# A sixteen-head, six-layer local-attention kernel: all scores of a half step in one run, the values of both heads in one run at its end, v's pieces together, k's norms of the second half in mid-step

## The chip, the cores and the metric

The kernel runs on one core of a Trainium2 chip. The time is device microseconds of that core for one execution of the whole program. The core has five engines with a queue each: PE (matrix products), DVE (vector work), ACT (activations and copies), POOL (more vector work) and SP, which here does nothing but issue DMAs. An engine takes its queue in order: an instruction that waits holds up all those behind it.

## The reference, cut to what matters

Sixteen sequences of 256 tokens with 128 features go through one causal attention layer (stage one of the kernel, which the change does not touch) and then through six layers of local attention and a gated feed-forward block (stage two):

```python
for i in range(DEPTH):                       # 6 layers
    x = attn_layer(shift_tokens(x), Wqkv[i], q_scale[i], k_scale[i], Wo[i]) + x
    x = ffn_layer(shift_tokens(x), ln_g[i], ln_b[i], W1[i], b1[i], W2[i], b2[i]) + x

# attn_layer: 16 heads of 64 features, windows of 32 tokens
q = l2norm(q) * qs;  k = l2norm(k) * ksc
q = q * cos * scale + rotate_half(q) * sin * scale
k = k * cos / scale + rotate_half(k) * sin / scale
sim = einsum('bhwie,bhwje->bhwij', bq, look(bk)) * 8   # own window and the one before
attn = softmax(where(mask, -max, sim), -1)
out = einsum('bhwij,bhwje->bhwie', attn, look(bv))
```

`look` joins each window with the window before it. All of it is in 32-bit floats.

## The kernel before, in words

Stage two handles 96 items n (six layers times sixteen sequences), one step each. A step has two halves, u = 0 and u = 1. Around item n the steps are a software pipeline: in step n the kernel projects q and k of item n + 2 (`proj_qk`, L463 to L477), finishes the norms of item n + 1 (`sums`, `roots`, `spread_k`, `norm_k`), computes the scores of item n (`sim`, L583), and projects the attention's result of item n - 1 (`project_out`, L666, which the profile calls wo). The heads are taken in four groups g of four (NG = 4); in every half, two of the four score tiles of an item, i = 2u and j = 2u + 1, are handled. The feed-forward block takes two sequences at a time (512 columns), spread over two steps: `glu_shift`, `glu_center` (cen), `glu_var` (pv), `glu_norm` (rs), `glu_part` (hg, ha) and `glu_out` (w). Which of them stands in a half depends on whether n is even, so the pattern repeats every pair of steps, that is every four halves.

The parts that the change and the prediction touch:

- `proj_qk` makes a PSUM tile `qk`; ACT squares it (L464), DVE multiplies it by the rotary tables into `t` (L465), POOL adds squares and turned parts (L474, L477) into `sq` and `tq`.
- `sums` (called n in the profile) adds the squares on PE (L484) and ACT copies the sums out. `roots` transposes them (nT, L495); DVE takes the inverse root in eleven small operations (nx, then rn and nz, L499 to L508); POOL spreads the result (kb, L511).
- `spread_k` transposes kb to a PSUM tile bc (L522), two groups at a time. `norm_k` multiplies the two k tiles by it on DVE (L536) and issues four DMAs on SP (L538) from `tq` to `us`, the layout that the scores read. `us` has three buffers.
- `masks` writes the mask into the PSUM tile of the scores (L563), `sim` adds the products of one group (64 small matmuls of two groups come to about 0.8 us). `soften` scales by q's and k's roots and subtracts the maximum (DVE L595, L603, POOL L604), `power` is the exponential (ACT, L610), `share` divides by the sum (DVE L617, L618; L620 on POOL or DVE).
- `attn_T` transposes the weights (aT, L626, copied by ACT at L628), `attn_v` multiplies by the values (po, L646, copied by ACT at L655).
- `proj_v` makes one of two pieces c of v for half u (v, L546); ACT copies it to `vn`, and SP issues DMAs that move it by one window to `vs` (L553, and for c = 0 also L555). `attn_v` reads both.

The order of the work is written out by hand in `half`. `in_order` pins it on PE, DVE, ACT and POOL: each instruction there gets an order-only dependence on the one before it on its engine. SP is not pinned; the framework's planner places the DMAs, and weight loads come as early as their buffers allow. PSUM tiles come from two pools: four slots for everything that `psum1` makes, two wider ones for scores and values (`psum2`). A tile waits for the last reader of the tile that had its slot.

Of the kernel before, what the change touches and what calls it, by code (L numbers as in the profile page):

```python
# [21 lines left out]
NG = HEADS // 4  # L22
# [16 lines left out]
def tile_transformer(  # L39
# [316 lines left out]
    with ExitStack() as st:  # L356
# [18 lines left out]
        def psum1(name):  # L375
            return ps_o.tile([P, 512], F32, tag="o", name=name)
# [115 lines left out]
        def roots(n, n2):  # L492
            ps = psum1(f"nT_{n}").rearrange("p (h g m) -> p h g m", h=4, g=4)
            for h in range(2):
                nc.tensor.transpose(  # L495
                    ps[:, h].rearrange("p g m -> p (g m)"), n2[:, h].rearrange("p a m -> p (a m)"), ident
                )
            x = p2.tile([P, 2, NG, 8], F32, tag="nx", name=f"nx_{n}")
            nc.vector.tensor_scalar(x, ps[:, 0:2, :, 0:8], 1e-24, None, ALU.max)  # L499

            y = p3.tile([P, 2, NG, 8], F32, tag="rn", name=f"rn_{n}")
            x_, y_ = (v.rearrange("p h g m -> p (h g m)") for v in (x, y))
            nc.vector.tensor_scalar(y_.bitcast(I32), x_.bitcast(I32), -0.5, 1597463007.0, ALU.mult, ALU.add)
            for _ in range(3):
                z = p4.tile([P, 64], F32, tag="nz", name=f"nz_{n}")
                nc.vector.tensor_tensor(z, x_, y_, ALU.mult)
                nc.vector.scalar_tensor_tensor(z, z, -0.5, y_, ALU.mult, ALU.mult)
                nc.vector.scalar_tensor_tensor(y_, z, 1.5, y_, ALU.add, ALU.mult)  # L508
            rn[n] = y
            kb = p1.tile([P, 2, NG, P], F32, tag="kb", name=f"kb_{n}")  # L510
            nc.gpsimd.tensor_copy(  # L511
                kb.rearrange("p h g (i d) -> p (h g) i d", d=32),
                y.rearrange("p h g m -> p (h g) m")[:, :, 4:8].unsqueeze(3).to_broadcast([P, 8, 4, 32]),
            )
            kbs[n] = kb
# [160 lines left out]
        def glu_shift(m):  # L676
            b = m % 8
            x2 = x2s[m] = p1.tile([P, 2 * S], F32, tag="gl", name=f"x2_{m}")
            for i in range(2):
                shifted(x2[:, i * S : (i + 1) * S], 2 * b + i)  # L680

        def glu_center(m):
            x2 = x2s.pop(m)
            ps = psum1(f"cen_{m}")
            nc.tensor.matmul(ps, center, x2, start=True, stop=True)
            sq2 = p1.tile([P, 2 * S], F32, tag="h1", name=f"fsq_{m}")
            nc.scalar.activation(sq2, ps, AF.Square)
            xc = p1.tile([P, 2 * S], F32, tag="h2", name=f"xc_{m}")
            nc.scalar.copy(xc, ps)
            xns[m] = sq2, xc  # L690

        def glu_var(m):
            sq2, xc = xns[m]
            pv = psum1(f"pv_{m}")
            for t in range(4):
                nc.tensor.matmul(pv[:, t : t + 1], sq2[:, t * P : (t + 1) * P], mean1, start=True, stop=True)
            var = p4.tile([P, 4], F32, tag="var", name=f"var_{m}")
            nc.vector.tensor_scalar(var, pv[:, :4], 1e-5, None, ALU.add)
            rstd = p4.tile([P, 4], F32, tag="rstd", name=f"rstd_{m}")
            rsqrt(rstd, var)  # L700
            xns[m] = rstd, xc

        def glu_norm(m):
            l = m // 8
            rstd, xc = xns[m]
            ps = psum1(f"rs_{m}")
            for t in range(4):
                nc.tensor.matmul(
                    ps[:, t * P : (t + 1) * P],
                    rstd[:, t : t + 1].to_broadcast([P, P]),  # L710
                    ident,
                    start=True,
                    stop=True,
                    is_transpose=True,
                )
            xn = p1.tile([P, 2 * S], F32, tag="xn", name=f"xn_{m}")
            nc.vector.tensor_tensor(xn, ps, xc, ALU.mult)
            nc.gpsimd.tensor_scalar(xn, xn, vecs[:, l, V_G : V_G + 1], vecs[:, l, V_B : V_B + 1], ALU.mult, ALU.add)
            xns[m] = xn

        def glu_part(mm, i):
            l = mm // 8
            if mm % 8 == 0 and i == 0:
                load_glu(l)
            xn = xns[mm]
            a, m = DI_PARTS[i]
            pg, ph = psum1(f"hg_{mm}_{i}"), psum1(f"ha_{mm}_{i}")
            nc.tensor.matmul(pg[:m], W["1"][:, DI + a : DI + a + m], xn, start=True, stop=True)  # L728
            nc.tensor.matmul(ph[:m], W["1"][:, a : a + m], xn, start=True, stop=True)  # L729
            g = p1.tile([P, 2 * S], F32, tag="gl", name=f"g_{mm}_{i}")  # L730
            nc.scalar.activation(g[:m], pg[:m], AF.Gelu, bias=vecs[:m, l, V_B1 + 3 + i : V_B1 + 4 + i])
            h = p1.tile([P, 2 * S], F32, tag=f"h{i}", name=f"h_{mm}_{i}")
            nc.vector.scalar_tensor_tensor(
                h[:m], ph[:m], vecs[:m, l, V_B1 + i : V_B1 + i + 1], g[:m], ALU.add, ALU.mult
            )
            hs[mm, i] = h
# [8 lines left out]
        def leave(s):  # L745

            ps = psum1(f"fin_{s}")
            for t in range(2):
                c0 = (s % 2) * S + t * P
                nc.tensor.transpose(ps[:, t * P : (t + 1) * P], yT[s // 2][:, c0 : c0 + P], ident)  # L750
            res = p2.tile([P, 2, E], F32, tag="res", name=f"res_{s}")
            nc.sync.dma_start(res, out[s].rearrange("(t p) e -> p t e", p=P))
            nc.vector.tensor_tensor(res, ps[:, :S].rearrange("p (t e) -> p t e", t=2), res, ALU.add)
            nc.sync.dma_start(out[s].rearrange("(t p) e -> p t e", p=P), res)
# [6 lines left out]
        def has(n):  # L761
            return 0 <= n < N

        def do(n, f, *a):
            if has(n):
                f(n, *a)
# [6 lines left out]
        def half(n, u):  # L773
            even = n % 2 == 0
            m = n // 2 - 1 if even else (n - 3) // 2
            glu = lambda m: 0 <= m < N // 2
            i, j = 2 * u, 2 * u + 1
            b, bu = (n, 0) if u else (n - 1, 1)
            bi, bj = 2 * bu, 2 * bu + 1
            do(b, share, bi)  # L780
            do(b, share, bj)
            do(n, sim, u, 0)
            do(n, sim, u, 1)
            for k in range(2):
                do(n + 2, proj_qk, i, k)
            if u == 0:
                do(n + 1, sums)
            elif not even and glu(m):
                glu_norm(m)
            do(n, sim, u, 2)  # L790
            do(n, sim, u, 3)
            do(n, soften, i)
            do(n, soften, j)
            do(n - 1, project_out, u)
            if u:
                do(n + 3, shift)
                if even and glu(m):
                    glu_shift(m)
            elif has(n + 1):
                roots(n + 1, n2s.pop(n + 1))  # L800
            do(b, attn_T, bi)
            do(b, attn_T, bj)
            do(n, proj_v, u, 0)
            do(b, attn_v, bi)
            if not even and u == 0 and glu(m):
                glu_center(m)
            do(n + 2, proj_qk, j, 0)
            if even and u == 0 and glu(m - 1):
                glu_part(m - 1, 2)
            if not even and glu(m):  # L810
                if u == 0:
                    glu_var(m)
                else:
                    glu_part(m, 0)
                    glu_part(m, 1)
            do(n + 2, proj_qk, j, 1)
            do(n + 1, spread_k, u)
            do(n + 1, norm_k, u)
            do(n, power, i)
            do(n, power, j)  # L820
            do(b, attn_v, bj)
            do(*((n, masks, 1) if u == 0 else (n + 1, masks, 0)))
            if even and u and glu(m - 1):
                glu_out(m - 1)
                if m - 1 >= (DEPTH - 1) * 8:
                    leave(2 * ((m - 1) % 8))
                    leave(2 * ((m - 1) % 8) + 1)
            do(n, proj_v, u, 1)

        last = {}  # L830
# [17 lines left out]
        for n in range(-2, N + 3):  # L848
            for u in range(2):
                traced = len(nc.cur_bb.bb.instructions)  # L850
                half(n, u)
                in_order(traced, 0 <= n < N)
# [97 lines left out]
```

## Time and profile before

| | |
|---|---|
| Median of 3 runs | 3765.55 us (3759.4 to 3772.61) |
| Profiled execution | 3770.29 us, span 3768.5 us |
| Granted TensorE clock, mean | 0.981 |
| PE busy | 3540.0 us, 94% |
| DVE busy | 2782.3 us, 74% |
| POOL busy | 2537.4 us, 67% |
| ACT busy | 1889.9 us, 50% |
| DMA, mean rate | 88 GB/s |
| PE idle before sim, until `us` landed | 107.2 us in 62 waits |

Stage one and the change to stage two take about the first 450 us; from there on the pattern of four halves repeats. A busy time is the sum over an engine's instructions; waits are given with the instruction that waited, and the one whose end released it. A pair of steps can be read half by half from the first `sim` of one half to the first `sim` of the next.

### The profile page before, as it was taken

The page shows a single profiled execution, that of the slowest core. Times are in us where ns is not written, and L with a number is a line of the kernel's source. Part 1 is how long each engine was busy: PE and PEld are TensorE (multiplying, and loading weights), DVE is VectorE, ACT ScalarE, POOL GpSimd, SP SyncE. Part 2 cuts the span into 40 slices and gives each one's busy share as a digit, 9 for nine tenths or more (in the row PEclk, how much of TensorE's full clock was granted, in tenths as well). Part 3 has the DMA queues.
Part 4 walks back from the last instruction along what each step waited for, and adds up shares of the span by engine and source line. Part 5 has one row for each costly group of instructions (what it writes and reads, how often), then busy time and mean ns, then how long its engine had stood idle before and what let it go on. Part 6 is the DMA issues. An engine that isn't in the chain of part 4 may idle for free.

```text
span 3768.5 us, 153634 instructions
## 1 busy us (share of the span) xinstructions
PE 3540.0 (94%) x68032; PEld 2482.4 (66%) x68032; DVE 2782.3 (74%) x4882; ACT 1889.9 (50%) x3180; POOL 2537.4 (67%) x2667
## 2 busy tenths in 40 slices
PE   8888799999999999999999999999999999999998
PEld 6666566666666666666666666666666666666665
DVE  5455677887877887777877778887777787777773
ACT  4444345555555554555554555555555555555453
POOL 1000577777777777777777777777777777777772
PEclk9999899999999999999999999999999999999998
DMA  2000233334333334333334333334333343333332
GB/s 79 6 8 8 68 99 84 97 96 105 105 93 96 88 95 106 103 95 86 96 99 105 94 102 88 93 94 105 105 87 96 86 104 93 107 91 96 102 96 63
DMA packets 249445, 331.66 MB, mean 88 GB/s; under 512 B 74446, under 2 KB 105548, under 8 KB 247884
## 3 DMA queue, kind: packets, MB, share of 16 engines
q1 hardware_dynamic: 248060, 321.13, 31.9%
q8 instruction: 536, 8.78, 1.0%
q14 instruction: 129, 1.06, 0.1%
q10 hardware_dynamic: 720, 0.70, 0.1%
HBM read 28.12 MB, written 4.19 MB: 9 GB/s over the span
## 4 chain that ended last, share of the span: by engine, by line
PE 75%; DMA 10%; DVE 5%; ACT 4%; issue 2%; POOL 2%; SPq 1%; ACTq 0%; DVEq 0%; POOLq 0%
PE qk L463 16%; PE po L646 9%; PE wo L666 9%; PE v L546 8%; DMA us<-tq 7%; PE sim L583 6%; PE w L742 4%; DMA vs<-vn 3%; PE hg L728 3%; PE ha L729 3%; PE aT L626 3%; PE bc L522 2%; PE st L222 1%; SPq L538 1%; ACT ex L269 1%
## 5 line engine op out<-in xcount | busy, mean ns | idle before, releaser
L465 DVE TENSOR_TENSOR t<-qk,ab 128x1024 f32<-128x1024 f32 x768 | 916.1, 1218 | 411.3 <-ACT sq L464 364.9
L477 POOL TENSOR_TENSOR tq<-t 128x512 f32<-128x512 f32 x768 | 961.0, 1272 | 105.9 <-DVE t L465 66.0
L463 PE MATMUL qk<-xs,wqk 128*128 128x256 f32 x3072 | 789.3, 393 | 0.4 <-DVE yT L671 0.2
L474 POOL TENSOR_TENSOR sq<-sq 128x512 f32<-128x512 f32 x384 | 488.4, 1272 | 341.9 <-ACT sq L464 335.5
L464 ACT ACTIVATE sq<-qk 128x512 f32<-128x512 f32 x768 | 459.2, 598 | 391.3 <-PE qk L463 380.9
L463 PEld LDWEIGHTS qk<-xs,wqk 128*128 128x128 f32 x3072 | 554.5, 190 | 145.7 <-issue 46.4
L628 ACT COPY aT<-aT 128x512 f32<-128x512 f32 x384 | 207.7, 586 | 689.9 <-PE aT L626 689.1
L583 PEld LDWEIGHTS sim<-us 64*32 64x32 f32 x24576 | 259.3, 106 | 327.1 <-issue 200.0
L646 PEld LDWEIGHTS po<-aT,vs 64*64 64x64 f32 x12288 | 327.0, 134 | 192.6 <-issue 107.2
L546 PE MATMUL v<-wv,xs 128*128 128x512 f32 x768 | 420.0, 629 | 20.7 <-ACT aT L628 20.5
L583 PE MATMUL sim<-us 64*32 64x64 f32 (+1 forms) x24576 | 330.8, 223 | 107.9 <-DMA us<-tq 107.2
L604 POOL TENSOR_TENSOR sm<-sm,mx 128x512 f32<-128x512 f32 x384 | 393.9, 1043 | 35.1 <-DVE mx L603 34.7
L666 PE MATMUL wo<-ao,wout 128*128 128x256 f32 x1536 | 408.5, 411 | 1.0 <-ACT ao L655 1.0
L646 PE MATMUL po<-aT,vs 64*64 64x32 f32 x12288 | 395.5, 222 | 10.0 <-DMA vs<-vn 8.7
L646 PE MATMUL po<-aT,vn 64*64 64x32 f32 x12288 | 387.1, 219 | 0.0
L552 ACT COPY vn<-v 128x512 f32<-128x512 f32 x384 | 225.0, 586 | 304.6 <-PE v L546 300.4
L620 POOL TENSOR_TENSOR ex<-ex,rec 128x512 f32<-128x512 f32 x288 | 317.0, 1115 | 33.5 <-ACT vn L552 17.9
L646 PEld LDWEIGHTS po<-aT,vn 64*64 64x64 f32 x12288 | 329.4, 135 | 0.0
L666 PEld LDWEIGHTS wo<-ao,wout 128*128 128x128 f32 x1536 | 292.2, 200 | 56.3 <-issue 2.5
L595 DVE TENSOR_TENSOR sm<-sim,rn 128x512 f32<-128x512 f32 x384 | 261.4, 681 | 80.9 <-PE sim L583 80.8
L655 ACT COPY ao<-po 128x512 f32<-128x512 f32 x384 | 222.6, 580 | 119.4 <-PE po L646 119.4
L603 DVE TENSOR_REDUCE mx<-sm 128x8 f32<-128x512 f32 x384 | 263.5, 686 | 13.2
(122 smaller groups left out, 5200.8 us busy)
## 6 DMA issues: line engine op xcount, KB each, us to landing
us<-tq SPq DMA_DIRECT2D x768, 256.0 KB
vs<-vn SPq DMA_DIRECT2D x384, 192.0 KB
vs<-vn SPq DMA_DIRECT2D x192, 64.0 KB
wqk<-in_f_wqkv_dram SPq DMA_DIRECT2D x96, 64.0 KB
ab<-in_tables_dram SPq DMA_DIRECT2D x6, 1024.0 KB
wv<-in_f_wqkv_dram SPq DMA_DIRECT2D x12, 256.0 KB
wout<-in_f_wo_dram SPq DMA_DIRECT2D x24, 128.0 KB
x<-in_x_dram SPq DMA_DIRECT2D x16, 128.0 KB
```

The lines of the kernel that those rows point to most:

```text
L463: nc.tensor.matmul(ps[:, t * S : t * S + S], W["qk", g][:, k, t, :], xs[n], start=True, stop=True)
L464: nc.scalar.activation(sq2[:, k].rearrange("p t n -> p (t n)"), ps, AF.Square)
L465: nc.vector.tensor_tensor(t12[:, k].rearrange("p f t n -> p f (t n)"), ps.unsqueeze(1).to_broadcast([P, 2, 2 * S]), W["ab", l][:, k].rearr ...
L474: nc.gpsimd.tensor_tensor(sq[n, g], sq2[:, :, 0, :], sq2[:, :, 1, :], ALU.add)
L477: nc.gpsimd.tensor_tensor(tq[n, g][:, t], t12[:, :, 0, t, :], t12[:, :, 1, 1 - t, :], ALU.add)
L546: nc.tensor.matmul(ps, xs[n][:, P * c : P * c + P], W["v"][:, u].rearrange("p g x d -> p (g x d)"), start=True, stop=True)
L583: nc.tensor.matmul(ps[WIN * r : WIN * r + WIN, x, col + first : col + 64], qk[part, g, 0, WIN * c : WIN * c + WIN], qk[part, g, 1, WIN * ( ...
L603: nc.vector.tensor_reduce(mx, seg, AX.X, ALU.max)
L604: nc.gpsimd.tensor_tensor(seg, seg, mx.unsqueeze(2).to_broadcast([P, 8, 64]), ALU.subtract)
L620: on.tensor_tensor(seg, seg, rec.unsqueeze(2).to_broadcast([P, 8, 64]), ALU.mult)
L646: nc.tensor.matmul(po[DH * y : DH * y + DH, h, x, g, WIN * r : WIN * r + WIN], v[64 * h : 64 * h + 64, r // 2, 2 * g + y, x, :], aT[64 * h ...
L666: nc.tensor.matmul(ps[:, :S].rearrange("p (h m) -> p h m", h=2), W["out"][:, g, 2 * u + x, :], a[:, x, :, g, :], start=(j == 0), stop=(j == 3)
```

## The change

Only `half` changes, and in it only the order of calls. All four groups of `sim` stand together at the start of a half; before, two stood ahead of the projections and two behind. `spread_k(n + 1, 1)` and `norm_k(n + 1, 1)` move from the end of the u = 1 half to the place behind the first two projections; those of u = 0 stay near the end. `attn_T` moves ahead of `project_out`. `attn_v` of the first tile moves to the end, directly ahead of that of the second, and the first piece of `proj_v` to the very end, directly ahead of the second piece.

```diff
             do(b, share, bi)
             do(b, share, bj)
-            do(n, sim, u, 0)
-            do(n, sim, u, 1)
+            for g in range(NG):
+                do(n, sim, u, g)
             for k in range(2):
                 do(n + 2, proj_qk, i, k)
             if u == 0:
                 do(n + 1, sums)
-            elif not even and glu(m):
-                glu_norm(m)
-            do(n, sim, u, 2)
-            do(n, sim, u, 3)
+            else:
+                do(n + 1, spread_k, 1)
+                do(n + 1, norm_k, 1)
+                if not even and glu(m):
+                    glu_norm(m)
             do(n, soften, i)
             do(n, soften, j)
+            do(b, attn_T, bi)
+            do(b, attn_T, bj)
             do(n - 1, project_out, u)
...
             elif has(n + 1):
                 roots(n + 1, n2s.pop(n + 1))
-            do(b, attn_T, bi)
-            do(b, attn_T, bj)
-            do(n, proj_v, u, 0)
-            do(b, attn_v, bi)
...
             do(n + 2, proj_qk, j, 1)
-            do(n + 1, spread_k, u)
-            do(n + 1, norm_k, u)
+            if u == 0:
+                do(n + 1, spread_k, 0)
+                do(n + 1, norm_k, 0)
             do(n, power, i)
             do(n, power, j)
+            do(b, attn_v, bi)
             do(b, attn_v, bj)
             do(*((n, masks, 1) if u == 0 else (n + 1, masks, 0)))
...
+            do(n, proj_v, u, 0)
             do(n, proj_v, u, 1)
```

## The prediction

> **What bounds the kernel now.** I read the page first (PE 94% busy of 3768.5 us, no other engine over 74%), then what PE waits for, then the busy time in the four halves of one pair of steps. In the waits the columns are total us, times, longest.
>
> ```profile
> PE sim L583 <- DMA us<-tq: 107.2, 62, 4.8
> ...
> PE po L646 <- DMA vs<-vn: 8.7, 20, 1.5
> ...
> PE bc L522 <- POOL kb L511: 5.8, 4, 3.0
> ```
>
> The change aims at the first two rows: 116 us of idle PE at most. The third row is small today; it is the one to watch.
>
> ```profile
> 2190.00:2206.50 16.50, 16.26 (x335) 11.61 (x335) 13.62 (x27) 8.09 (x15) 12.14 (x12) 1.00 0.32 90
> 2206.50:2223.40 16.90, 16.90 (x324) 11.87 (x326) 13.32 (x20) 10.08 (x15) 13.13 (x14) 1.00 0.34 91
> 2223.40:2242.30 18.90, 16.25 (x329) 10.99 (x328) 13.87 (x28) 10.26 (x17) 12.49 (x12) 1.00 0.30 83
> 2242.30:2258.40 16.10, 15.81 (x316) 11.08 (x316) 12.71 (x19) 7.38 (x14) 14.05 (x20) 1.00 0.44 111
> ```
>
> Each row is one half (length, then busy PE, weight loads, DVE, ACT, POOL, clock, DMA). In order: odd step u=0 (call it O0), odd u=1 (O1), even u=0 (E0), even u=1 (E1). PE fills three of them; E0 holds the wait for `us`. DVE has 13 to 14 us of work in each: it is not the bound, but it has little room to catch up. From the `us` wait near 573 us to the one near 3606 us lie 44 pairs: 68.92 us a pair on average, half-clock time included.
>
> Now the chain behind the third row, in O0 (start us, us, engine, line). Its first sim starts at 2189.99.
>
> ```profile
> 2190.68 1.99 PE L463 MATMUL qk<-xs,wqk 128*128 128x256 f32 x8
> 2194.38 1.99 PE L666 MATMUL wo<-ao,wout 128*128 128x256 f32 x8
> 2196.21 0.38 PE L495 MATMUL nT<-cst,n 128*128 128x128 f32 x2
> 2203.50 0.60 PE L522 MATMUL bc<-cst,kb 128*128 128x128 f32 x4
> ...
> 2192.61 2.36 DVE L465 TENSOR_TENSOR t<-qk,ab 128x1024 f32<-128x1024 f32 x2 [1.08 <-ACT sq L464]
> ...
> 2197.85 0.21 DVE L499 TENSOR_SCALAR nx<-nT 128x64 f32<-128x64 f32 x1
> ...
> 2201.48 0.22 DVE L508 SCALAR_TENSOR_TENSOR rn<-nz,rn 128x64 f32<-128x64 f32 x1
> ...
> 2201.84 1.04 POOL L511 COPY kb<-rn 128x1024 f32<-128x1024 f32 x1 [2.29 <-PE qk L463]
> ```
>
> DVE goes without a pause from t (2192.61) through soften and yT to the inverse roots (2197.85 to 2201.70); POOL then spreads them into kb, ready at 2202.88; PE's bc comes at 2203.6. So kb is ready 12.1 us after the i projections start, and bc arrives 0.8 us later. The slack is 0.8 us. Where DVE once ran late, bc did wait:
>
> ```profile
> 3130.64 1.03 PE L463 MATMUL qk<-xs,wqk 128*128 128x256 f32 x4
> 3132.97 0.63 PE L522 MATMUL bc<-cst,kb 128*128 128x128 f32 x4 [1.29 <-POOL kb L511]
> ```
>
> **The change part by part.** No work is added or removed. Everything is an order within PE's, DVE's, ACT's and SP's queues.
>
> *k's norms of u=1 to mid-step.* `tq` is multiplied after t (5.7 us into the half) until 6.9; four issues take 2.9 us (the row of SP's four us<-tq issues), landing takes 5.4 to 5.7 (chain of waits), so the last piece is there by some 15 us, and the next half's sims start at 17.7 or later. The wait for `us` goes: 2.4 us in the pair shown, 107.2 us in all. SP: these four issues now stand ahead of the v pieces and, at layer starts, ahead of weight loads; nothing needs those sooner.
>
> *v together, values together, at the end.* vs of a half is needed by the next half's po, 8.5 us in; its three issues end 2.5 us in and land 5 us later, at 7.7. Covered by 0.8 us, so the 8.7 us go too.
>
> *Transitions on PE.* Eight qk or wo matmuls cost 1.92 us behind the sims but 8 x 0.215 = 1.72 inside a run; the first full-width group behind po also costs 0.2 more (1.06 against 0.86). The new order has two such edges fewer in a half: 0.4 us, 1.6 a pair.
>
> *What the order costs: u=0 halves.* Two things happen to the chain above. All four sims (1.54) stand ahead of qk, so qk, t, the roots and kb come 0.77 us later: kb at 1.54 + 12.1 = 13.65. And v (0.86) and the first po (1.06), which stood between nT and bc and covered the roots, now stand behind bc. PE reaches bc at 1.54 sim + 1.92 qk + 1.00 n + 0.87 aT + 1.72 wo + 0.22 nT + 3.6 (cen, qk, pv, qk; in E0 qk, hg, ha, qk) = 10.9. It waits 2.8 us. Queued behind bc on PE are po, po, masks, v, v and the next half's sims: 0.44 + 2.12 + 0.34 + 1.05 + 0.86 = 4.8 us that nothing else needs sooner, but that all have to run before the next half's qk starts DVE again. Hence O0 = 13.7 + 4.8 = 18.5 us (16.5 now). E0's roots took 3.3 us instead of 3.85 in this trace: 18.3 (18.9 now with its wait).
>
> *What it costs: u=1 halves.* Here kb is long ready, but bc, aT and wo come early and reuse PSUM slots that DVE has not read. By the built program's slots, in O1 the first aT waits for t of the first qk (arrives 4.35, free 4.65: 0.3), the second aT for the ACT copy of the first (0.65), hg for POOL's xn (0.2): 16.45 + 1.15 = 17.6 (16.9 now). In E1 only 0.3: 15.2 + 0.3 = 15.5 (16.1 now). DVE's extra work before soften (1.28) delays yT to 10.6, which hg of the second part reaches at 10.7: no further wait.
>
> Sum of a pair at full clock: 18.5 + 17.65 + 18.3 + 15.5 = 69.95.
>
> *The clock.* Idle PE costs more than the idle time (first PE's timeline, then the stretches before and after that gap, the clock third from the end):
>
> ```profile
> 2159.90 0.49 PE L583 MATMUL sim<-us 64*32 64x32 f32 x32 [2.65 <-DMA us<-tq]
> 2160.32 3.60 PE L666 MATMUL wo<-ao,wout 128*128 128x256 f32 x8
> ```
>
> ```profile
> 2153.90:2160.10 6.20, 3.55 (x85) 2.32 (x88) 3.37 (x6) 1.99 (x4) 4.99 (x5) 1.00 0.77 205
> 2160.10:2163.70 3.60, 3.60 (x40) 2.82 (x20) 2.66 (x4) 0.00 (x0) 3.10 (x4) 0.53 0.00 0
> ```
>
> After a gap of 2.65 us the granted clock was 0.53 and wo took 3.60 us instead of 1.92. Of the 21 gaps of 2.1 to 2.8 us that PE's records of stage two show, 11 were followed by half clock, of 4.03 us on average: 2.0 us lost each; of the gaps near 1 us hardly any. The Trainium skill (TensorE: Matmul & The Clock Gate, Part 1) says that the clock falls after an idle window of about 3.4 us: by that rule a gap of 2.8 us never lowers it and the loss is zero, or 4.0 us a pair at the most if every gap did. I take the row: 11/21 x 2.0 x 2 gaps = 2.1 us a pair.
>
> *Layer starts.* There POOL multiplies the tables (two of 1.9 us) and t came 3 us late; today part of this hides in the `us` wait of that half. In the new order it lengthens the wait at bc by about 3.6 us and makes half clock sure: 5.6 us for eight pairs, 0.7 a pair. (Today's layer-start pairs are some 6 us long too; they are in the 68.92.)
>
> Total 69.95 + 2.1 + 0.7 = 72.75 against 68.92: 3.8 us more a pair. With 46 pairs in steady state 176 us on the profiled execution (span 3768.5, its time 3770.3). The median of the runs shown, 3765.55, lies 4.7 below that; added to it: **3940 us**.
>
> **The rivals.** *Bc waits, the clock hardly falls* (the rule): 69.95 + 0.3 + 0.3 for layer starts, +1.65 a pair, 3840. For it: 10 of 21 gaps kept full clock. *The clock falls after nearly every gap*: +2 us a pair, about 4030. For it: new gaps are at the upper end of the 21, and of the 8 longer than 2.5 us 6 had half clock.
>
> *Faster: bc does not wait.* If kb came in time, u=0 halves would take about 15.7 us each: 15.7 + 17.65 + 15.7 + 15.5 = 64.55, with 0.3 for layer starts 4.1 less a pair, 3580. The point of decision: at full clock and with 0.7 for layer starts the two waits together must fall from 5.35 to below 3.6 us, so kb must come 0.9 us earlier in each half. Against it: t, soften, yT and the roots stand in the same order in DVE's queue as before, and DVE had no pause in them. For it: the second to third root operation took 1.0 us where the others took 0.23, while POOL was at work beside it; if that overlap goes, 0.8 us is won.
>
> *The change does not remove the wait for `us`*: it would add up to 107 us to any of these. The landing has 2 us to spare, so I give it no share of its own.
>
> **How the numbers follow.** Forecast (bc waits, about half of the gaps at half clock) 0.58; clock hardly falls 0.15; clock nearly always falls 0.12; bc hardly waits and the kernel is faster 0.11; gains and waits cancel 0.04. Range 3820 to 4010: it takes in the second case and most of the third. A difference under 0.3% (11 us) can't be told from none; faster 0.11, same 0.04, slower 0.85.
>
> **What would show it.** Right: PE sim <- us gone from PE's waits (under 15 us); PE bc <- POOL kb at 200 us or more, some 96 times, up to about 3 us each; u=0 halves of 18 to 19 us, O1 17.5, E1 15.5; aT <- ACT aT about 0.6 us in O1; more stretches at half clock; PE's wo at 1.72 behind aT. Wrong: if bc's wait is under 1.5 us each, kb came sooner and the kernel is faster; if `us` still heads the list, the mid-step issue was held up on SP; if the clock stays at 0.98 or above, less than half of the forecast's loss is left.

## The result, and the profile after

The changed kernel takes 4702.48 us, median of 4 runs (4695.84 to 4704.83). The kernel before took 3764.16 us beside it (4 runs). The ratio is 1.2487, with a 95% interval of 1.2461 to 1.2513: a quarter slower. The forecast was 3940 us with a range that ended at 4010. The direction was right, the size was wrong by a factor of more than five: 938 us more where 176 were expected.

The first page of the profile after, parts 1 and 2 (busy time of each engine, then the granted clock in 40 slices of the span, in tenths):

```profile
PE 3981.6 (85%) x68032; PEld 2728.4 (58%) x68032; DVE 2818.0 (60%) x4882; ACT 1927.6 (41%) x3180; POOL 2542.1 (54%) x2667
...
PEclk9998888888888888888888888888888888888888
```

DVE, ACT and POOL have the same busy time as before, within 2%. PE is busy for 442 us more with the same number of matmuls, and idle for 721 us where it was idle for 228. So there are two losses: PE waits more, and it works more slowly. The mean clock is 0.859 (0.981 before).

What PE waits for (total us, times, longest):

```profile
PE po L646 <- ACT ao L655: 292.7, 192, 3.8
PE bc L522 <- POOL kb L511: 267.9, 96, 6.5
PE aT L626 <- DVE t L465: 36.4, 94, 0.7
PE aT L626 <- ACT aT L628: 31.1, 46, 0.7
...
PE sim L583 <- DMA us<-tq: 6.2, 4, 3.4
```

The last row is what the change set out to remove, and it did: 107.2 us became 6.2. The second row is the wait that the forecast named. The first row, the largest, is not in the forecast at all.

The busy time in the four halves of a pair, O0, O1, E0 and E1 as before (length, then busy PE, weight loads, DVE, ACT, POOL, clock, DMA share, GB/s):

```profile
2603.00:2626.20 23.20, 19.79 (x314) 13.66 (x305) 15.41 (x30) 7.91 (x15) 14.77 (x13) 0.78 0.24 66
2626.20:2650.00 23.80, 20.05 (x320) 12.98 (x319) 12.55 (x18) 10.88 (x16) 13.11 (x14) 0.86 0.24 65
2650.00:2673.30 23.30, 19.83 (x331) 13.25 (x330) 15.61 (x28) 10.50 (x16) 11.54 (x10) 0.79 0.30 81
2673.30:2691.40 18.10, 15.65 (x318) 11.31 (x320) 10.34 (x15) 7.05 (x12) 12.14 (x17) 0.98 0.33 91
```

Every half got longer, by 2.0 to 6.9 us. The pair takes 88.4 us. E1 keeps nearly the full clock and PE is busy there for as long as before (15.65 us against 15.81): what it lost is idle time alone. The other three lost both.

Here is the first wait, from the timeline of O1 (start us, us, engine, line; in brackets the idle time before it and what ended it; other rows are left out, marked by dots):

```profile
2640.26 0.60 ACT L464 ACTIVATE sq<-qk 128x512 f32<-128x512 f32 x1 [0.51 <-PE qk L463]
...
2640.88 1.28 ACT L610 ACT_TABLE_LOAD   x1
...
2642.17 1.15 ACT L610 ACTIVATE ex<-sm 128x512 f32<-128x512 f32 x2
...
2643.23 0.56 ACT L655 COPY ao<-po 128x512 f32<-128x512 f32 x1
...
2643.85 0.44 PE L646 MATMUL po<-aT,vs 64*64 64x32 f32 x8 [2.56 <-ACT ao L655]
```

`attn_v` of both tiles writes the same PSUM tile `po`, each into its own columns. ACT copies the first part to `ao` before the second part is issued (L655), so the copy stands between the two products, and the second product waits for it. With the two products side by side on PE nothing covers that copy. On ACT it stands behind `sq`, a load of the exponential's table and two exponentials: 2.56 us of idle PE in this half.

And the second loss: the stretches around the two gaps of O0 and O1 (columns as above, the clock third from the end):

```profile
2613.50:2616.30 2.80, 0.14 (x1) 0.00 (x0) 2.59 (x10) 1.63 (x3) 1.04 (x1) 0.97 0.00 0
2616.30:2626.50 10.20, 9.45 (x177) 5.95 (x178) 5.22 (x9) 1.99 (x4) 6.17 (x5) 0.51 0.40 108
2626.50:2641.30 14.80, 13.60 (x233) 9.56 (x213) 10.09 (x14) 7.00 (x11) 7.69 (x10) 1.00 0.37 101
2641.30:2643.80 2.50, 0.00 (x0) 0.00 (x0) 1.75 (x4) 2.48 (x4) 2.50 (x3) 0.93 0.02 7
2643.80:2650.30 6.50, 6.45 (x102) 3.42 (x109) 0.71 (x2) 1.38 (x3) 2.92 (x3) 0.50 0.03 7
```

The gap before `bc` is followed by 10.2 us at half clock, the gap before the second `po` by 6.5 to 6.8. Behind the gaps of before, the forecast had read 4.0 us on average. From 460 us on, the records hold 148 stretches at half clock, 1283 us in all (88 of 10.2 us, 52 of 6.8, 8 of 3.4); before there were 21, with 105 us. All such totals below are counted from 460 us on.

### The profile page after: what moved, and what is told of

It is laid out like the page before. It is cut to its first block, busy times and chain, and to the rows that moved or that the text cites. A ratio compares the mean times of both kernels' runs of the same rounds, so it can differ in the third digit from the quotient of the medians.

```text
span 4703.0 us, 153371 instructions
## 1 busy us (share of the span) xinstructions
PE 3981.6 (85%) x68032; PEld 2728.4 (58%) x68032; DVE 2818.0 (60%) x4882; ACT 1927.6 (41%) x3180; POOL 2542.1 (54%) x2667
## 4 chain that ended last, share of the span: by engine, by line
PE 53%; DVE 27%; ACT 13%; POOL 4%; issue 3%; DMA 0%; DVEq 0%; ACTq 0%; POOLq 0%; SPq 0%
PE v L546 13%; PE po L646 11%; DVE t L465 8%; PE sim L583 6%; PE qk L463 6%; DVE mx L603 4%; DVE sm L595 4%; ACT sq L464 4%; DVE nz L506 3%; PE w L742 3%; ACT ao L655 2%; POOL kb L511 2%; PE sim L563 2%; PE bc L522 2%; PE wo L666 2%
## 5 line engine op out<-in xcount | busy, mean ns | idle before, releaser
L646 PE MATMUL po<-aT,vs 64*64 64x32 f32 x12288 | 547.0, 265 | 292.7 <-ACT ao L655 292.7
L646 PEld LDWEIGHTS po<-aT,vs 64*64 64x64 f32 x12288 | 443.0, 184 | 379.5 <-ACT ao L655 316.2
L546 PE MATMUL v<-wv,xs 128*128 128x512 f32 x768 | 628.7, 965 | 0.0
L646 PE MATMUL po<-aT,vn 64*64 64x32 f32 x12288 | 539.5, 262 | 0.0
L655 ACT COPY ao<-po 128x512 f32<-128x512 f32 x384 | 222.8, 580 | 665.6 <-PE po L646 665.6
L646 PEld LDWEIGHTS po<-aT,vn 64*64 64x64 f32 x12288 | 454.9, 188 | 0.0
L522 PE MATMUL bc<-cst,kb 128*128 128x128 f32 x768 | 153.6, 335 | 267.9 <-POOL kb L511 267.9
L666 PE MATMUL wo<-ao,wout 128*128 128x256 f32 x1536 | 363.6, 379 | 0.0
L546 PEld LDWEIGHTS v<-wv,xs 128*128 128x128 f32 x768 | 203.8, 289 | 252.8 <-issue 231.2
L583 PE MATMUL sim<-us 64*32 64x64 f32 (+1 forms) x24576 | 308.4, 235 | 6.2 <-DMA us<-tq 6.2
L522 PEld LDWEIGHTS bc<-cst,kb 128*128 128x128 f32 x768 | 106.5, 165 | 316.4 <-POOL kb L511 306.7
```

The source lines that it names most:

```text
L522: nc.tensor.transpose(ps[:, g].rearrange("p (a h m) -> p h a m", a=2, h=2)[:, h], kbs[n][:, h, 2 * j + g, :], ident)
L546: nc.tensor.matmul(ps, xs[n][:, P * c : P * c + P], W["v"][:, u].rearrange("p g x d -> p (g x d)"), start=True, stop=True)
L583: nc.tensor.matmul(ps[WIN * r : WIN * r + WIN, x, col + first : col + 64], qk[part, g, 0, WIN * c : WIN * c + WIN], qk[part, g, 1, WIN * ( ...
L646: nc.tensor.matmul(po[DH * y : DH * y + DH, h, x, g, WIN * r : WIN * r + WIN], v[64 * h : 64 * h + 64, r // 2, 2 * g + y, x, :], aT[64 * h ...
L655: nc.scalar.copy(ao[n, u][:, x], po[:, :, x])
L666: nc.tensor.matmul(ps[:, :S].rearrange("p (h m) -> p h m", h=2), W["out"][:, g, 2 * u + x, :], a[:, x, :, g, :], start=(j == 0), stop=(j == 3)
```

## The experiments

Two theories stood against each other. T1: idle gaps on PE are the cause of both losses; each gap costs its own time and half of the stretch at half clock behind it, so a removed gap gives back more than its wait. T2: the clock is low for a reason of its own in the new order, and a removed wait gives back the wait alone. In the expectations T2 also names what its reason might be: long runs of small matmuls. A third, T3, put a loss on the scores in one run and the early norms themselves.

**The copies behind both products.** The new `po` wait is taken away at its root: both copies are issued once both products are done, so no reader stands between them.

```diff
-            nc.scalar.copy(ao[n, u][:, x], po[:, :, x])
+            if x == 1:
+                for y in range(2):
+                    nc.scalar.copy(ao[n, u][:, y], po[:, :, y])
```

> The changed kernel, but both copies of a half's values are issued behind both products, so that the second product no longer waits for the first copy. Theory T1 (idle PE lowers the clock, and stretches at half clock of 7 to 10 us are the larger part of the loss): the 292.7 us of po <- ACT ao go, the half clock behind po in odd steps goes (6.8 us of it a pair), the gap at bc and its half clock stay. 6 + 3.4 to 6.8 us a pair less: 4250 to 4130. Rival T2 (the half clock comes from long runs of small matmuls, not from gaps): only the waits go, 4702 - 293 = 4410, and the mean clock stays near 0.86.

Measured: 4147.69 us, 1.1012 (1.0988 to 1.1037) of the time before. The row of `po` is gone; `bc` is as it was:

```profile
PE bc L522 <- POOL kb L511: 266.8, 96, 6.2
```

A wait of 293 us gave back 555 us. The rest is the clock, 0.922 now, with 607 us at half clock. It falls in T1's range; T2's 4410 is far off.

**The other wait.** `spread_k` and `norm_k` of u = 0 are moved behind the values, so that `bc` comes later.

```diff
             do(n + 2, proj_qk, j, 1)
-            if u == 0:
-                do(n + 1, spread_k, 0)
-                do(n + 1, norm_k, 0)
...
             do(b, attn_v, bj)
+            if u == 0:
+                do(n + 1, spread_k, 0)
+                do(n + 1, norm_k, 0)
```

> The changed kernel, with spread_k and norm_k of u = 0 behind the values instead of ahead of them, the wait for kb covered by the values. T1: bc no longer waits, but the second po of u = 0 halves now waits for the copy of the first, which stands behind the exponentials on ACT: about 2.5 us of gap in the place of 2.7 + 0.7. 4550 to 4720, hardly better. If the wait at bc were the cause by itself: 5.5 us of wait and up to 10 us of half clock a pair less, below 4100. T2: 4702 - 100 to 300.

Measured: 4374.7 us, 1.1615 (1.1589 to 1.1641). The wait at `bc` went, and reappeared one instruction group further:

```profile
PE po L646 <- ACT ao L655: 396.3, 192, 3.8
```

That shift was expected, the gain of 328 us was not: T1's range began at 4550, and T2's reached down to 4402, nearer to the result. The waits fell by only about 156 us in sum (259 less at `bc`, 104 more at `po`). The time at half clock fell from 1283 to 792 us, because its stretches are shorter: none of 10.2 us, 88 of 6.8, 55 of 3.4. The number of stretches is nearly the same (144). How long a stretch lasts is thus not set by the number of gaps alone.

**Both edits together.**

> Both edits together: no wait left at bc and at po. T1: clock back to 0.97 or more, a pair of 65 to 67 us, 3580 to 3700, faster than both kernels. T2: the waits go, the clock stays near 0.86: 4702 - 560 = 4140.

Measured: 3719.35 us, 0.9873 (0.9855 to 0.989). 983 us come back for two edits of order that add and remove no work, and the clock is 0.990 (36 us at half clock). This refutes T2's 4140. It stays a little above T1's range, since `bc` moved late still waits a little:

```profile
PE bc L522 <- POOL kb L511: 78.4, 94, 6.3
```

**More work in the gap.** If idleness lowers the clock, useless work in the gap must make the changed kernel faster. Six full-width matmuls go into `bc`'s PSUM tile ahead of its transposes; their results are overwritten.

```diff
+            if j == 0:
+                for _ in range(6):
+                    nc.tensor.matmul(ps[:, 0], ident, xs[n], start=True, stop=True)
```

> The changed kernel with six idle-time matmuls (128x256, results overwritten, about 2.6 us together) ahead of the transposes bc of u = 0 halves: PE is busy where it waited for kb; nothing else changes, more work is done and no wait is shortened. T1: the half clock behind bc goes or shrinks to that of the second gap, 10 us of half clock in each u = 0 half, so up to 10 us a pair less: 4250 to 4500. T2: no gain, 4700 or a little more.

Measured: 4400.82 us, 1.1684 (1.1655 to 1.1714): 302 us less than the changed kernel, with more work. The timeline of PE at that place shows how (the filler is the second row; it moves the lines behind it by three, so `v` is L549 here):

```profile
2623.14 1.11 PE L463 MATMUL qk<-xs,wqk 128*128 128x256 f32 x4
2624.08 2.75 PE L522 MATMUL bc<-xs,cst 128*128 128x256 f32 x12
2626.96 0.66 PE L525 MATMUL bc<-cst,kb 128*128 128x128 f32 x4
...
2630.78 1.98 PE L549 MATMUL v<-wv,xs 128*128 128x512 f32 x4
```

The filler takes as long as the wait did, so `bc` comes no sooner. But the four `v` matmuls behind it take 1.98 us; in the changed kernel they take 3.78:

```profile
2612.53 1.11 PE L463 MATMUL qk<-xs,wqk 128*128 128x256 f32 x4
2616.34 1.11 PE L522 MATMUL bc<-cst,kb 128*128 128x128 f32 x4 [2.70 <-POOL kb L511]
...
2620.03 0.44 PE L646 MATMUL po<-aT,vs 64*64 64x32 f32 x8 [0.70 <-ACT ao L655]
...
2622.45 3.78 PE L546 MATMUL v<-wv,xs 128*128 128x512 f32 x4
```

The `po` waits did not change (290.3 us), and half clock fell to 399 us. The order of the real work is the same and only the idleness is gone: idle PE is what lowers the clock at this place; this is shown.

**The parts of the change alone, on the kernel before.** First the scores in one run and the norms of u = 1 in mid-step.

> The kernel before with one part of the change alone: the four groups of scores in one run, and k's norms of u = 1 in mid-step; values, v and attn_T stay where they were. Theory T1 (the loss comes from the values moved behind bc and put back to back): the wait for us goes (2.2 us a pair), one change of matmul shape a half is saved (0.8 a pair), kb comes 0.77 us later and just uses up the slack of 0.8 at bc: 3 us a pair less, 3620 to 3680. Rival T3 (the scores ahead of the projections delay DVE's chain enough to make bc wait by itself): waits at bc above 1 us in u = 0 halves and half clock, 3800 or more.

Measured: 3733.21 us, 0.9898 (0.9874 to 0.9922). T3 is false, but the gain is 38 us by the ratio of times, less than half of the least that was expected (86). The wait for `us` (101 us) and 82 us of half clock (worth 35 in PE's busy time) went. New small waits took some of it:

```profile
PE v L546 <- ACT aT L628: 31.9, 134, 0.2
PE bc L522 <- POOL kb L511: 25.7, 49, 5.2
...
PE wo L666 <- DVE t L465: 15.6, 46, 0.3
```

Against before these are 47 us more. Another 15 us are pauses before `sim` of the kind found below with `v` behind `bc` (37 here). And PE's own work got 28 us longer: its busy time fell by 7 us only, not by 35; `qk` and `aT` take 39 us more, for a reason that isn't settled. 101 + 35 - 47 - 15 - 28 = 46, and the span fell by 37.

Next the values alone: `attn_v` of the first tile directly ahead of that of the second, nothing else.

> The kernel before with another part alone: the values of both tiles back to back at the end of the half. T1: the second po waits for the copy of the first, which stands behind the exponentials on ACT: 2.5 us in the two halves with table loads, about 1 us in the others, and half clock behind the longer ones (some 7 us each): 12 us a pair more, about 4300; bc waits only 0.3 us. T3: near 3766.

Measured: 4020.92 us, 1.0667 (1.0635 to 1.07). This one move is enough to turn the sign.

```profile
PE po L646 <- ACT ao L655: 231.6, 192, 2.7
PE bc L522 <- POOL kb L511: 63.6, 94, 4.6
```

The size was overestimated, by about 280 us: the stretches at half clock are mostly of 3.4 us here (59 of 70, 272 us in all), where some 7 were expected.

Then `v`'s pieces alone, both at the end of the half.

> The kernel before with v's two pieces together at the end of the half. T1: bc loses 0.9 us of cover, about its slack; the wait for us in even steps stays: 3750 to 3810. T3: the same.

Measured: 3815.73 us, 1.0123 (1.0086 to 1.016). A small loss, slightly above the range that both theories gave, so it does not tell them apart: the `us` wait shrank, but three others took its place.

```profile
PE sim L583 <- DMA us<-tq: 60.8, 36, 5.6
PE po L646 <- DMA vs<-vn: 41.3, 69, 1.8
PE po L646 <- ACT aT L628: 40.9, 163, 0.8
PE bc L522 <- POOL kb L511: 31.3, 70, 4.2
```

The row of `vs` bears on a step of the forecast: `v` at the end does come late for `po` where the rest of the half is in the old order.

**What sets the length of a stretch.** In the changed kernel the `bc` gap is followed by 128 of the small `po` matmuls, with a second gap of 0.7 us among them; in the kernel before, a gap was followed by 32 small matmuls and then full-width `wo`. Here both pieces of `v`, full width, are put directly behind `bc`:

```diff
+            do(n, proj_v, u, 0)
+            do(n, proj_v, u, 1)
             do(b, attn_v, bi)
             do(b, attn_v, bj)
...
-            do(n, proj_v, u, 0)
-            do(n, proj_v, u, 1)
```

> The changed kernel with v's two pieces directly behind bc, ahead of the values: the gap at bc stays (2.7 us), but full-width matmuls follow it in the place of 128 small ones. If the stretch at half clock lasts as long as the work behind the gap is small matmuls, it falls from 10.2 to about 3.4 us in u = 0 halves: up to 6.8 us of run time a pair less, 4390 or more. If a gap of this length costs 10 us of half clock whatever follows: 4650 to 4720.

Measured: 4558.54 us, 1.2094 (1.2059 to 1.2129). Timeline and stretches around one `bc`:

```profile
2619.25 0.77 PE L522 MATMUL bc<-cst,kb 128*128 128x128 f32 x4 [2.71 <-POOL kb L511]
2619.81 3.51 PE L546 MATMUL v<-wv,xs 128*128 128x512 f32 x4
2623.24 0.32 PE L646 MATMUL po<-aT,vs 64*64 64x32 f32 x8
...
2625.09 0.32 PE L646 MATMUL po<-aT,vs 64*64 64x32 f32 x8 [0.71 <-ACT ao L655]
...
2629.69 0.49 PE L583 MATMUL sim<-us 64*32 64x64 f32 x21 [1.88 <-issue]
```

```profile
2619.40:2622.00 2.60, 2.60 (x7) 1.42 (x7) 2.60 (x4) 0.24 (x1) 2.60 (x3) 0.55 0.00 0
2622.00:2627.80 5.80, 5.09 (x245) 3.32 (x243) 2.47 (x5) 2.10 (x4) 3.48 (x3) 0.91 0.67 195
```

The gap is the same 2.7 us, and the clock is back soon after 2622, where in the changed kernel it stayed at half for 10.2 us. Over the run, 102 of 150 stretches are of 3.4 us and 6 of 10.2; the total fell from 1283 to 692 us. So the work behind a gap decides how long half clock lasts. The second gap, of 0.7 us, is still there (2625.09), only later; and with the copies behind both products, where it is gone, 34 stretches of 10.2 us remain. So it is not what makes a stretch long. A count over all traces, further down, points to the width of the work. The first of the two expectations thus holds, though in time it gave only a lower bound (4390 or more).

The gain in time is only 144 us, in part because a new gap arose within the scores, of 1.6 us on average. The view of waits names no instruction or transfer that ends it:

```profile
PE sim L583 <- issue: 179.0, 115, 3.3
```

The trace does. PE's own instructions come in blocks, over a queue of their own (transfers, MB, share of the 16 DMA engines):

```profile
q8 instruction: 534, 8.75, 0.8%
```

That is 534 transfers of 16,384 bytes. 534 times 256 is 136,704, and PE has 136,775 records (matmuls and weight loads), so a block holds 256 of them (in the kernel before, 536 times 256 is 137,216, with 137,218 records). From one of the 115 pauses to the next, PE's records count a multiple of 256 each time, to within 3, and every one of the pauses ends 1.1 to 1.7 us after the end of such a transfer (a moment taken at random does so in 7% of cases). So PE has used up its instructions and waits for the next block. The order makes this likely: `po`, the masks and the scores are over 500 records in about 4 us, and two transfers start at least 3.3 us apart. In the changed kernel `v` stands between them, and there is no such pause.

**A version that beats both.** With the copies behind both products, and `bc` of u = 0 late, something should cover the rest of the roots. Two orders: `bc` of u = 0 behind the masks and the first piece of `v`; or, with `bc` behind the masks, that piece of `v` back in mid-half where it was before the change.

> The changed kernel with both copies behind both products, as in e3_both, and bc of u = 0 halves another 1.4 us later on PE, behind the masks and v's first piece. T1: the 0.7 us that bc still waited in every u = 0 half of e3_both goes, 1.5 us a pair: 3719 - 65 = 3655, if k's norms do not come too late for DVE's next half.

> As e3_both, but v's first piece stays in mid-half, where it covers the roots, and bc stands behind the masks: scores, norms and values are grouped, v is not. T1: no wait at bc, one more edge of shapes on PE saved than in e6_scores_norms_alone: 3650 to 3700, below e3_both (3719) and e6 (3733).

The second, as an edit of the changed kernel beside that of the copies:

```diff
+            do(n, proj_v, u, 0)
...
             do(n + 2, proj_qk, j, 1)
-            if u == 0:
-                do(n + 1, spread_k, 0)
-                do(n + 1, norm_k, 0)
...
             do(*((n, masks, 1) if u == 0 else (n + 1, masks, 0)))
+            if u == 0:
+                do(n + 1, spread_k, 0)
+                do(n + 1, norm_k, 0)
...
-            do(n, proj_v, u, 0)
             do(n, proj_v, u, 1)
```

Measured: 3665.13 us for the first (0.9739, 0.9718 to 0.976) and 3652.54 us for the second (0.9705, 0.9684 to 0.9726, 5 runs). Both beat both kernels; the first misses its 3655 by 10 us, the second lies in its range. What PE still waits for in stage two of the second:

```profile
PE aT L626 <- DVE t L465: 52.5, 93, 1.0
PE aT L626 <- ACT aT L628: 31.1, 46, 0.7
PE sim L583 <- issue: 27.0, 49, 1.9
```

The last row is again PE waiting for blocks of its instructions: all 49 pauses end 1.1 to 1.7 us after such a transfer.

## Why the prediction was right in direction and wrong in size

**Right.** `bc` waits for `kb`: 2.8 us in O0 and about 2.55 in E0 were forecast, the records give 267.9 us in 96 waits, 2.8 on average. The chain through t, the roots and POOL and the cover that was moved away were read rightly. The wait for `us` is gone (6.2 us left), and so is that for `vs`. In both u = 1 halves the first `aT` waits for t (0.3 forecast, 36.4 us in 94 waits measured), and in O1 the second for ACT's copy of the first (0.65 forecast, 31.1 us in 46 waits, 0.68 each). `wo` behind `aT` takes 1.73 us (1.72 forecast, at full clock). The wait of `hg` for POOL's xn, 0.2 us, was not seen. Two readings are slightly off, without effect on the result: by the rows shown the slack before `bc` was 0.6 us (2202.88 to 2203.50), not 0.8, and O1 is 17.6 in the working but 17.65 in the sum.

**Wrong: "v together, values together, at the end".** This step asked one question only, whether `vs` has landed, and closed with "covered by 0.8 us". It missed what stands between the two products: ACT's copy of the first. Before, two projections, `bc` and, in three of the four halves, feed-forward work lay between them. With the values together that reader is in the path: 292.7 us in 192 waits, 6.1 us a pair, where the sum had nothing (its "po, po" are 2.12 us without a pause). The forecast costed the DMA that feeds the moved instruction, and not the reader of the tile that it writes into. The values alone (1.0667) show that this move by itself makes the kernel slower, and the copies behind both products show that the reader between is the cause: its row disappears.

**Wrong, and larger: the clock.** The term was 11/21 x 2.0 us x 2 gaps = 2.1 us a pair. Three factors were too small. The number of gaps: three a pair lowered the clock, not two, since the `po` gap of O1 counts too. The share: 92 of the 92 gaps of 2.3 to 3.0 us before `bc`, and 46 of the 48 before `po`, have half clock beside them, not 11 of 21. And the length: 10.2, 6.8 and 10.2 us, where 4.03 was taken. That is 27.2 us a pair at half clock and 13.6 lost, more than six times the term. The rival "nearly always" changed the share only, so it came no further than 4030. The length was taken from gaps that were followed by wide `wo` matmuls, without asking what would follow the new ones.

The rule that the forecast weighed, an idle window of about 3.4 us (the Trainium skill, TensorE: Matmul & The Clock Gate, Part 1), would have let all these gaps of 2.3 to 3.0 us pass. The measurement decides against it as the forecast read it. The traces do show such a window, but it need not be idle throughout. In each of the twelve traces the granted clock changes only on a fixed grid in time, with a step of 3.413 us, to within 7 ns. Call one step a cell. This is how the clock of a cell went with PE's work in the cell before it, counted over all twelve. PE is busy where the records say so, with the modelled ends of matmuls; full-width matmuls are those with 128*128 in the profile's rows; cells at half clock in which PE pauses for more than 3% are left out.

| the cell before | cells | next cell at half clock |
|---|---|---|
| full clock, PE busy under 40% of it | 470 | 470 |
| full clock, PE busy 40 to 60% | 330 | 202 |
| full clock, PE busy 60% or more | 10,508 | 52 |
| half clock, PE busy 97% or more, full-width matmuls under 40% of the cell | 155 | 130 |
| half clock, PE busy 97% or more, full-width matmuls 40% or more | 673 | 1 |

The counts are of what goes together; the runs that changed one thing on purpose (the filler, and `v` behind `bc`) agree with them. They explain three things. Idleness starts half clock, if enough of it falls into one cell: a gap of 2.7 us is four fifths of one. Small matmuls then keep it, with PE busy all the while, and a cell with enough full-width work ends it. So T2 was wrong on the start (of 489 cells at full clock with PE busy 90% or more and full-width matmuls under 40%, none led to half clock) and partly right on the length. And the length of a gap alone is no threshold: of the 2.0 to 2.3 us gaps before `po` in the changed kernel 4 of 46 had half clock, but 39 of 49 with the values alone, and 45 of 46 with `bc` late. In the changed kernel only 1 of the 46 had four fifths of its length in one cell; with `bc` late 44 had.

**The account.** Four kernels against before, in us of the profiled spans. Half clock counts as half of the difference in PE's busy time at half clock (a wait is no longer for it); edges are the forecast's own 1.6 us for each of 48 pairs, an estimate that no run measured alone.

| | changed | copies after | bc late | both |
|---|---|---|---|---|
| po for ACT's copy | +293 | 0 | +396 | 0 |
| bc for kb | +262 | +261 | +3 | +73 |
| aT for t and ACT | +67 | +67 | +68 | +69 |
| us | -101 | -101 | -101 | -101 |
| vs, and v for aT | -29 | -29 | -27 | -26 |
| edges (estimate) | -77 | -77 | -77 | -77 |
| pauses for PE's instructions | 0 | +22 | 0 | +20 |
| half clock | +545 | +239 | +334 | -30 |
| sum | +960 | +382 | +596 | -72 |
| measured, spans | +935 | +377 | +603 | -51 |

Two columns close within 7 us. The changed kernel comes out 25 us better than its sum and the version with both edits 21 worse; these remainders are open. The extra time at layer starts (0.7 us a pair in the forecast) could not be told from the rest.

## What to carry to other kernels

When two writers of one PSUM tile are moved together, list every reader that stands between them, and what stands ahead of that reader on its own engine: the second writer waits for all of it. Price a new idle gap on PE by the gap and by the half-clock stretch behind it, and take that stretch from a place where the same kind of work follows; here it ran from 3.4 to 10.2 us for the same 2.7 us gap. Count PE's busy share by cells of the clock's grid rather than by the length of the gap. And before a consumer is pulled forward, count the work that was its cover: here the fix was to put `bc` behind work that nobody waits for.

## What the runs showed of the hardware that was not expected

Half clock begins and ends on a grid of 3.413 us, so its stretches are of 3.4, 6.8 or 10.2 us. A loop can lock to that grid: in the changed kernel 74 of the 92 times from a `bc` gap to the same one a pair later lie between 88.6 and 88.9 us, with a median of 88.74, and 26 steps of the grid are 88.75. There the gaps fall at nearly the same place in a cell, pair after pair: 80 of 92 gaps before `bc` begin between one and three tenths into it.

Full-clock cells with PE busy under 40% were followed by half clock in 470 of 470 cases, and small matmuls held half clock in 130 of 155 cells in which PE was busy for 97% or more. Gaps of 2.3 to 3.0 us on PE cost up to three times their length, and useless matmuls in the gap made the kernel 302 us faster.

Long runs of small matmuls can use up PE's instructions faster than they come. Every one of the 115 pauses within the scores, with `v` behind `bc`, lies a multiple of 256 records from the last and ends 1.1 to 1.7 us after a transfer of 16,384 bytes on PE's instruction queue (179 us in all).
